# A cross-attention loop fused with two expert mixtures: each batch's turns, values and closing in the step behind its scores, and its row DMAs spread over more places

## The chip, the cores and the metric

The kernel runs on one core of a Trainium2 chip. The metric is the device time of one execution, in microseconds (us). The time of a kernel is the median of several runs. One more execution is recorded by the hardware profiler; its times are those of the profile.

## What is computed

Two layers work on x, 16 batches of 128 tokens by 256 features in float32, with a second sequence of the same shape as context. Cut to the parts that matter:

```python
x = x + tanh(g_xattn[0]) * mlstm(layernorm(x), ctx, ctx, ...)
x = x + tanh(g_ffn[0])   * mixture0(layernorm(x), ...)   # 8 experts, top 2, 2 shared experts
x = x + tanh(g_xattn[1]) * attention(layernorm(x), ctx, mask, ...)
x = x + tanh(g_ffn[1])   * mixture1(layernorm(x), ...)   # 16 experts in 4 groups, top 4, 1 shared expert

def attention(hq, hk, mask, Wq, bq, Wk, bk, Wv, bv):     # 16 heads of 16
    q, k, v = heads(hq @ Wq.T + bq), heads(hk @ Wk.T + bk), heads(hk @ Wv.T + bv)
    s = einsum('bhqd,bhkd->bhqk', q / sqrt(16), k) + (1 - mask)[:, None] * -10000.0
    return join_heads(einsum('bhqk,bhkd->bhqd', softmax(s), v))
```

The change touches only the third of these lines and what is woven into it: the end of mixture 0 (its rows are fetched back and added to x) and the beginning of mixture 1 (layer norm, shared expert, routing, sorting, and the scattering of rows to the experts' order).

## The kernel before

The stages follow each other: mLSTM and the shared experts of mixture 0; 39 tiles of mixture 0's experts; the attention loop, which this case is about; the expert tiles of mixture 1, a group of experts per tile, in two halves of the batches.

The 16 batches are in four groups g of GB = 4. The attention loop is a loop over steps b. Each engine executes its instructions in the order in which the program issues them, so the order of the calls in the loop is the order of the work ("manual schedule"); an engine waits at an instruction until what it needs is there. A step has these parts for a batch:

- scores(b): 16 matmuls of 32 rows each write four score tiles sp0 to sp3 in PSUM (L1001), four heads in each.
- softmax(b, r), r = 0 to 3: for each head, VectorE adds the mask and takes the row's extreme (L1014), then ScalarE takes the exponential (L1020). The result is a tile sc (7 buffers).
- turn(b, r): four TensorE transposes of sc into the PSUM tile tp (L1027), and a ScalarE copy to SBUF as pT (L1029, 4 buffers).
- values(b): 16 matmuls that use 32 columns of the array each, values times pT, into the PSUM tile cp (L1038), and a ScalarE copy as cT (L1043, 2 buffers). The values are widened by a column of ones, so that the row sums come along.
- close(b): four transposes of cT into the PSUM tile pv (L1051), on VectorE the reciprocal, a scaling and the product o (L1055 to L1058), and on GpSimd the addition of o to x (L1060).

In PSUM, the pool s3p has one buffer for each of sp0 to sp3, two buffers under the tag "tp" (tp, cp, pv, and the layer norm's ln_tp take turns in them) and two under the tag "e" (the results of big matmuls: qps, sgp, sup, yps, r1ps).

Into the steps, other work is woven as "units": at(step, place, (function, arguments)) files a unit under a step and one of its three places 0, 1, 2, and run(step, place) issues what is filed there. A place written as one number p stands for step p // 3, place p % 3. The units are:

- gather_b(b): two row DMAs on GpSimd (L678) that fetch mixture 0's rows of a batch; add_b(b): two VectorE operations that add them to x.
- ln_stats, apply3, ln_turn: a layer norm in three parts (VectorE and GpSimd; VectorE L324; transposes L336 on TensorE and copies L337 on ScalarE), once per group for the attention's queries ("q") and once for mixture 1 ("m").
- q_proj(g, o): four matmuls into qps (L985) and a VectorE operation (L989).
- shared4_gate: four matmuls into sgp (L1069) and a tanh on ScalarE (L1073). shared4_up: four matmuls into sup (L1079) and two VectorE operations, L1084 with the tanh and sgp, L1085 with sup; sgp's buffer is free after L1084. shared4_down: matmuls into yps (L1091) and a VectorE addition to x (L1095).
- pump(g): slices of the routing of a group (matmuls r1ps, L1103, a ScalarE operation, then a chain of VectorE operations). pump_sort(0): slices of the sorting of the first half's eight batches by expert group.
- scatter(0, k, j): a row DMA on GpSimd (L1254) that writes batch k's rows to their slots for one of two choices j. The first expert tile (xt, loaded by SyncE; transposed into xtp, L1286; multiplied, gu, L1301) reads what the scatters wrote.

In the kernel before, the step of scores(b) runs values(b-2) behind the scores, then in two halves: turn of two quarters of batch b-1, softmax of two quarters of batch b, and the units of one place; then close(b-2) and the units of place 2. So a batch takes part in three steps. SyncE's loads of keys, masks and values for later groups (L927, L931) are issued ahead of a step's scores.

The functions touched by the change and their callers:

Of the kernel before, what the change touches and what calls it, by code (L numbers as in the profile page):

```python
# [25 lines left out]
G = 4  # L26
GB = B // G
# [40 lines left out]
def flamingo_kernel(ctx: ExitStack, tc: tile.TileContext, a: dict, out: bass.AP):  # L68
# [87 lines left out]
    def tok(ap, g):  # L156
        return ap[g * GB : (g + 1) * GB].rearrange("b s d -> s b d")

    def bc(ap, shape):
        return ap.unsqueeze(len(shape) - 1).to_broadcast(shape)  # L160
# [540 lines left out]
    units = {}  # L701

    def at(step, place, *fs):
        units.setdefault((step, place), []).extend(fs)

    def run(step, place):
        for f, *args in units.pop((step, place), ()):
            f(*args)
# [7 lines left out]
    NB = G * GB  # L716
    ENG = {nc.tensor.engine, nc.vector.engine, nc.scalar.engine, nc.gpsimd.engine}
    for g in range(G):
        s0 = GB * g

        k1, k2 = (1, g), (2, g)
        s0 = GB * g - (g > 0)
# [8 lines left out]
        s0 = GB * g  # L731
# [164 lines left out]
    with tc.manual_schedule(engines=ENG):  # L896
        g = G - 1
# [24 lines left out]
    s3 = w3_stack.enter_context(tc.tile_pool(name="s3", bufs=2))  # L922
    s3p = w3_stack.enter_context(tc.tile_pool(name="s3p", bufs=1, space=PSUM))

    def load_k(g):
        kz_g[g] = s3.tile([P, KC, 2, TG], F32, tag="kz", name="kz")
        sync.dma_start(out=kz_g[g], in_=kz_d[g])  # L927

    def load_va(g, pr):
        va_g[g, pr] = s3.tile([P, 2, NH1, VW], F32, tag="va", name="va", bufs=3)  # L930
        sync.dma_start(out=va_g[g, pr], in_=va_d[g][:, 2 * pr : 2 * pr + 2])  # L931

    def new_mask():
        return s3.tile([P, GB, S], F32, tag="mb", name="mb")
# [31 lines left out]
    NR = P // VW  # L966
# [40 lines left out]
    def softmax(b, r, sp):  # L1007

        g, i = divmod(b, GB)
        sc = s3.tile([P, HQ, S], F32, tag="sc", name="sc", bufs=7)  # L1010
        mx = mx_b[b]
        for k in range(HQ):
            n = r * HQ + k
            nc.vector.tensor_tensor_reduce(  # L1014
                out=sc[:, k, :], in0=sp[:, k // 2, k % 2, :], in1=masks[g][:, i, :],
                scale=1.0, scalar=3.0e38, op0=ALU.add, op1=ALU.min, accum_out=mx[:, n : n + 1],
            )
        for k in range(HQ):
            n = r * HQ + k
            nc.scalar.activation(sc[:, k, :], sc[:, k, :], AF.Exp, scale=-1.0, bias=mx[:, n : n + 1])  # L1020
        sc_b[b, r] = sc

    def turn(b, r):
        sc = sc_b.pop((b, r))
        tp = s3p.tile([P, HQ, S], F32, tag="tp", name="tp", bufs=2)
        for k in range(HQ):
            nc.tensor.transpose(tp[:, k, :], sc[:, k, :], ident)  # L1027
        pT = s3.tile([P, HQ, S], F32, tag="pT", name="pT", bufs=4)
        nc.scalar.copy(pT, tp)  # L1029
        pT_b[b, r] = pT  # L1030

    def values(b):
        g, i = divmod(b, GB)
        cp = s3p.tile([P, NR, S], F32, tag="tp", name="cp", bufs=2)
        for r in range(NR):
            pT = pT_b.pop((b, r))
            for k in range(HQ):
                nc.tensor.matmul(  # L1038
                    cp[ts(k, VW), r, :], va_g[g, i // 2][:, i % 2, r * HQ + k, :], pT[:, k, :],
                    start=True, stop=True, tile_position=(0, k * VW),  # L1040
                )
        cT = s3.tile([P, NR, S], F32, tag="cT", name="cT")
        nc.scalar.copy(cT, cp)  # L1043
        cp_b[b] = cT

    def close(b):
        g, i = divmod(b, GB)
        cT = cp_b.pop(b)
        pv = s3p.tile([P, NH1, VW], F32, tag="tp", name="pv", bufs=2)
        for q in range(NR):  # L1050
            nc.tensor.transpose(  # L1051
                pv[:, ts(q, HQ), :].rearrange("p h d -> p (h d)"), cT[:, q, :], ident
            )
        rd = s3.tile([P, NH1], F32, name="rd")
        nc.vector.reciprocal(rd, pv[:, :, DH1])  # L1055
        nc.vector.tensor_scalar(rd, rd, tx1, None, ALU.mult)
        o = s3.tile([P, NH1, DH1], F32, name="o", bufs=1)
        nc.vector.tensor_tensor(o, pv[:, :, 0:DH1], bc(rd, [P, NH1, DH1]), ALU.mult)  # L1058
        xt = x_g[g][:, i, :]
        nc.gpsimd.tensor_tensor(xt, xt, o.rearrange("p h d -> p (h d)"), ALU.add)  # L1060
# [330 lines left out]
    for g in range(G):  # L1391
        q, m, s0 = ("q", g), ("m", g), GB * g
        for i in range(GB if g else 0):
            p = 3 * (s0 - 5) + i - 1 + 2 * (g == 1)
            at(*divmod(p, 3), (gather_b, s0 + i))
            at(*divmod(p + (4 if g == 1 else 2), 3), (add_b, s0 + i))
        if g == 0:
            at(-1, 0, (ln_turn, q, 0, s3p), (ln_turn, q, 1, s3p))
        else:
            n = 3 * (s0 - 3) + 2 * (g == 1)  # L1400
            at(*divmod(n, 3), (ln_stats, q, s3))
            at(*divmod(n + 1, 3), (apply3, q, 0))
            at(*divmod(n + 2, 3), (ln_turn, q, 0, s3p), (apply3, q, 1))
            at(*divmod(n + 3, 3), (ln_turn, q, 1, s3p))
        at(s0 - 1, 0, (q_proj, g, 0))
        at(s0 - 1, 1, (q_proj, g, 1))
        if g == G - 1:
            break
        at(s0 + 5, 2, (ln_stats, m, s3))
        at(s0 + 6, 0, (apply3, m, 0))  # L1410
        at(s0 + 6, 1, (ln_turn, m, 0, s3p), (apply3, m, 1))
        at(s0 + 6, 2, (ln_turn, m, 1, s3p))
        at(s0 + 7, 0, (shared4_gate, g, 0))
        at(s0 + 7, 1, (pump, g))
        at(s0 + 7, 2, (pump, g, 2))
        at(s0 + 8, 0, (pump, g, 2))
        at(s0 + 8, 1, (pump, g, 2))
        at(s0 + 8, 2, (pump, g))
        n = 3 * (s0 + 7) + 1
        for f in range(SC1):  # L1420
            at(*divmod(n + 2 * f, 3), (shared4_up, g, f))
            if f + 1 < SC1:
                at(*divmod(n + 2 * f + 1, 3), (shared4_gate, g, f + 1))
        n += 2 * SC1
        for t in range(0, GB, 2):
            at(*divmod(n + t // 2 - 1, 3), (shared4_down, g, t), (shared4_down, g, t + 1))
# [2 lines left out]
    ):  # L1429
        at(1 + b, 2, f)  # L1430

    at(13, 0, (pump_sort, 0, 1))
    at(13, 1, (pump_sort, 0, 2))
    at(13, 2, (pump_sort, 0, 2))
    at(14, 0, (pump_sort, 0, 2))
    at(14, 1, (pump_sort, 0, 2))
    for k in range(BH):
        at(14 + (k + 2) // 3, (k + 2) % 3, (scatter, 0, k, 0), (scatter, 0, k, 1))

    m = ("m", G - 1)
    at(GB * G + 1, 2, (ln_stats, m, s3))
    hooks = {
        0: [(apply3, m, 0), (apply3, m, 1)], 1: [(ln_turn, m, 0, s3p), (ln_turn, m, 1, s3p)],
        2: [(pump, G - 1, 1)], 3: [(pump, G - 1, 2)], 4: [(pump, G - 1, 2)], 5: [(pump, G - 1, 2)],
# [5 lines left out]
        hooks[NT1 + 4 + k] = [(gather, 0, k)]  # L1452

    with tc.manual_schedule(engines=ENG | {sync.engine}):
        for b in range(-1, NB + 3):
            if b >= 0 and b % GB == 0:
                if 0 < b < NB:
                    load_va(b // GB, 1)
            if b >= 0 and b // GB + 1 < G:
                g = b // GB + 1  # L1460
                if b % GB == 1:
                    load_k(g)
                elif b % GB == 2:
                    load_mask(g, new_mask())
                elif b % GB == 3:
                    load_va(g, 0)
            old = b - 1 if 0 < b <= NB else None
            sp = scores(b) if 0 <= b < NB else None
            if 0 <= b - 2 < NB:
                values(b - 2)  # L1470
            for hf in range(2):
                if old is not None:
                    turn(old, 2 * hf)
                    turn(old, 2 * hf + 1)
                for r in range(2 * hf, 2 * hf + 2):
                    if sp:
                        softmax(b, r, sp[r])
                run(b, hf)
            if 0 <= b - 2 < NB:
                close(b - 2)  # L1480
            run(b, 2)
    with tc.manual_schedule(engines=ENG):
        for i in range(NHF * NT1 + 2):
            tile_step(i)
            for f, *args in hooks.get(i, ()):
                f(*args)
        g, k = G - 1, 0
        for f in range(SC1):
            shared4_gate(g, f)
            shared4_up(g, f)  # L1490
            if f:
                gather(1, k)
                gather(1, k + 1)
                k += 2
        for t in range(GB):
            shared4_down(g, t)
            if k < BH:
                gather(1, k)
                k += 1
        for hf in range(NHF):  # L1500
            for g in range(hf * G // NHF, (hf + 1) * G // NHF):
                sync.dma_start(out=tok(out, g), in_=x_g[g])
# [83 lines left out]
```

## Time and profile before

| what | value |
|---|---|
| median of three runs | 984.41 us (980.81, 984.61, 984.41) |
| the profiled execution's own time | 979.63 us |
| its span in the profile | 977.9 us (1.7 us lie outside) |
| mean granted TensorE clock | 0.945 |
| instructions | 13890 |
| attention loop, first scores to the first matmul of mixture 1's tiles (gu) | 573.7 to 815.9 us, 242.2 us |
| length of the steps of scores 0 to 14 | 2.7, 7.8, 14.8, 14.8, 8.5, 11.1, 12.9, 23.1, 13.9, 14.5, 12.1, 15.9, 11.1, 13.3, 13.8 us |
| from the last scores to the first gu | 52.2 us |
| behind that, to the end | 162.0 us |

All times of the profile are counted from the start of the span. A step's length is the time from its first score matmul to the next step's. TensorE's row "PE" holds matmuls and "PEld" its weight loads, which lie beside matmuls; the granted clock is the part of full speed that TensorE was given, and at half clock (0.50) its matmuls take about twice as long. In a timeline line the numbers are the start, the duration of the stretch, the engine, the line, the operation, output and inputs, how many instructions the stretch holds, and in brackets how long the engine was idle before it and what released it.

### The profile page before, as it was taken

The numbers are of one execution on the slowest core, as the hardware profiler recorded it, in microseconds if no ns is written. First come the engines' busy times: TensorE is split into PE (matmuls) and PEld (weight loads), VectorE is DVE, ScalarE is ACT, GpSimd is POOL, SyncE is SP. The second block draws the span as 40 slices with busy tenths as digits, with TensorE's granted clock in tenths as the row PEclk, the third lists the DMA queues.
The fourth block names the chain that finished last, engine by engine and source line by source line (L and its number), as shares of the span: only waits on it lengthen the run. The fifth ranks groups of instructions, "written<-read, shape, count | busy, mean of one in ns | idle before, by whom it ended". The sixth has DMA issues, their size and how long they took to land. (4 is left out here: it accounts for less than half of the span.)

```text
span 977.9 us, 13890 instructions
## 1 busy us (share of the span) xinstructions
PE 860.3 (88%) x4432; PEld 535.9 (55%) x4432; DVE 472.2 (48%) x1731; ACT 394.0 (40%) x945; POOL 216.5 (22%) x316
## 2 busy tenths in 40 slices
PE   4778998999979999999999976768899679989996
PEld 2555556656545556566555644535656436555653
DVE  2496556554373222222222454838868344833634
ACT  2455655662102211211121145754666424444540
POOL 3023001110003111111110333231201241154515
PEclk9887999999999999999999977789999789999999
DMA  8998312100683111111110174120000012344613
GB/s 236 304 320 288 105 33 74 54 22 1 230 307 108 37 45 44 44 45 47 44 43 23 54 280 156 39 92 28 23 23 1 36 46 63 95 136 122 192 60 118
DMA packets 66390, 98.23 MB, mean 100 GB/s; under 512 B 9648, under 2 KB 49712, under 8 KB 65808
## 3 DMA queue, kind: packets, MB, share of 16 engines
q1 hardware_dynamic: 59840, 79.39, 24.8%
q0 software_dynamic: 6480, 17.97, 6.1%
q8 instruction: 37, 0.61, 0.3%
q14 instruction: 33, 0.27, 0.1%
HBM read 64.64 MB, written 32.69 MB: 100 GB/s over the span
## 5 line engine op out<-in xcount | busy, mean ns | idle before, releaser
L811 POOL DMA_INDIRECT xt<-xn_d,ti x39 | 39.8, 1021 | 209.5 <-PE xtp L826 164.3
L1020 ACT ACTIVATE sc<-sc,mx 128x128 f32<-128x128 f32 x256 | 78.3, 394 | 4.6 <-DVE mx L1014 4.6
L840 PE MATMUL tgp<-w1e,xT 128*128 x156 | 79.4, 593 | 0.0
L858 PE MATMUL typ<-w2e,thT 128*128 x312 | 76.9, 389 | 0.0
L1301 PE MATMUL gu<-wgu,xT 128*128 x152 | 73.8, 608 | 0.9 <-DVE xT L1288 0.5
L840 PE MATMUL tup<-w3e,xT 128*128 x156 | 73.3, 592 | 0.0
L858 PEld LDWEIGHTS typ<-w2e,thT 128*128 128x128 f32 x312 | 56.1, 189 | 31.2 <-ACT thT L855 25.1
L845 ACT ACTIVATE tsg<-tgp 128x512 f32<-128x512 f32 x39 | 23.3, 598 | 121.3 <-PE tgp L840 121.3
L847 DVE TENSOR_TENSOR h<-tup,tsg 128x512 f32<-128x512 f32 x39 | 27.0, 692 | 88.0 <-PE tup L840 85.4
L1027 PE MATMUL tp<-ident,sc 128*128 128x128 f32 x256 | 43.4, 310 | 28.1 <-ACT cT L1043 17.2
L519 PE MATMUL gp<-xnT,w 128*128 128x512 f32 x128 | 65.6, 636 | 0.0
L1014 DVE CUSTOM_DVE_ANT_0 sc<-sp,mb 128x128 f32<-128x128 f32 x256 | 56.3, 286 | 16.2 <-PE sp L1001 11.4
L530 PE MATMUL up<-xnT,w 128*128 128x512 f32 x128 | 60.8, 598 | 0.0
L540 PE MATMUL yp<-w,hT 128*128 128x256 f32 x256 | 58.4, 382 | 1.1 <-DVE hT L534 1.1
L862 DVE COPY ys<-typ 128x256 f32<-128x256 f32 x39 | 16.6, 426 | 87.5 <-PE typ L858 87.5
L1027 PEld LDWEIGHTS tp<-ident,sc 128*128 128x128 f32 x256 | 32.8, 159 | 44.7 <-ACT cT L1043 20.5
L534 DVE TENSOR_TENSOR hT<-up,sg 128x512 f32<-128x512 f32 x32 | 22.1, 691 | 69.6 <-PE up L530 39.7
L540 PEld LDWEIGHTS yp<-w,hT 128*128 128x128 f32 x256 | 47.7, 190 | 9.7 <-DVE hT L534 2.1
L678 POOL DMA_INDIRECT yg<-ys_d,si x32 | 33.5, 1047 | 85.9 <-DMA ys_d<-ys 43.0
L855 ACT COPY thT<-htp 128x512 f32<-128x512 f32 x39 | 22.9, 587 | 69.3 <-PE htp L853 69.3
L840 PEld LDWEIGHTS tup<-w3e,xT 128*128 128x128 f32 x156 | 29.6, 190 | 37.3 <-issue 37.1
L448 ACT ACTIVATE dm<-dm,gaT 128x128 f32<-128x128 f32 x128 | 40.5, 392 | 14.9 <-DVE dm L444 14.8
(281 smaller groups left out, 1600.8 us busy)
## 6 DMA issues: line engine op xcount, KB each, us to landing
dm<-m_d SPq DMA_DIRECT2D x16, 512.0 KB
xs<-zero SPq DMA_DIRECT2D x2, 2584.0 KB
xt<-xs SPq DMA_DIRECT2D x38, 136.0 KB
ys_d<-ys SPq DMA_DIRECT2D x39, 128.0 KB
ys<-ys SPq DMA_DIRECT2D x38, 128.0 KB
kz_d<-kst SPq DMA_DIRECT2D x8, 512.0 KB
va_d<-vs SPq DMA_DIRECT2D x8, 512.0 KB
w1e<-in_L_ffn_w_T_dram SPq DMA_DIRECT2D x8, 512.0 KB
```

Of the source, the lines that this page charges most:

```text
L448: nc.scalar.activation(t[:, h, :], t[:, h, :], AF.Exp, bias=gate_g[g][0][:, n : n + 1])
L519: nc.tensor.matmul(gp, shw[e][0][:, c, ts(f_, P)], xnT_g[2, g][:, c, :], start=(c == 0), stop=(c == KC - 1))
L530: nc.tensor.matmul(up, shw[e][1][:, c, ts(f_, P)], xnT_g[2, g][:, c, :], start=(c == 0), stop=(c == KC - 1))
L540: nc.tensor.matmul(yp, sh_g[g, e * HC0 + f][:, ts(t, P)], shw[e][2][:, f, :], start=(f == 0), stop=(f == HC0 - 1))
L678: nc.gpsimd.indirect_dma_start(out=yg, out_offset=None, in_=ys_d[:, :], in_offset=bass.IndirectOffsetOnAxis(ap=si_j[j][:, b : b + 1], axis=0),
L811: nc.gpsimd.indirect_dma_start(out=xt, out_offset=None, in_=xn_d[:, :], in_offset=bass.IndirectOffsetOnAxis(ap=ti[:, i : i + 1], axis=0), ...
L840: nc.tensor.matmul(ps, xT[:, c, :], w_[:, bass.ds(ev + c * HID0, HID0)], start=(c == 0), stop=(c == KC - 1),)
L858: nc.tensor.matmul(yp, hT[:, f, :], w2e[:, bass.ds(ev + f * D, D)], start=(f == 0), stop=(f == HC0 - 1))
L1014: nc.vector.tensor_tensor_reduce(out=sc[:, k, :], in0=sp[:, k // 2, k % 2, :], in1=masks[g][:, i, :], scale=1.0, scalar=3.0e38, op0=ALU.ad ...
L1020: nc.scalar.activation(sc[:, k, :], sc[:, k, :], AF.Exp, scale=-1.0, bias=mx[:, n : n + 1])
L1027: nc.tensor.transpose(tp[:, k, :], sc[:, k, :], ident)
L1301: nc.tensor.matmul(gu, xT[:, c, :], wgu[:, bass.ds(ev + c * NGRP * 2 * GW, 2 * GW)], start=(c == 0), stop=(c == KC - 1),)
```

## The change

Within the attention loop a batch takes part in two steps in place of three: in the step of scores(b) all four turns of batch b-1 follow the scores, then the softmax of three quarters of batch b, values(b-1), the fourth quarter's softmax, the units of places 0 and 1, close(b-1), and the units of place 2. The loop has one step fewer. On TensorE the order of a step is now scores, 16 transposes, cp's 16 matmuls, units, pv, units; before it was scores, cp's matmuls, 8 transposes, units, 8 transposes, units, pv, units. On ScalarE it is now four pT copies, twelve exponentials, cT, four exponentials, units; before it was cT, two pT copies, eight exponentials, units, two pT copies, eight exponentials, units.

The m units of the groups 0 to 2 (layer norm, shared expert, routing) are filed one step earlier, and the sort of the first half too. The q units stay where they are, so that in two steps a layer norm of each kind falls together. The gathers of groups 2 and 3 are filed at every second place, in place of four places in a row; those of group 1 stay. The 16 scatters are filed over ten places from step 13, place 2, to step 16, place 2; before, two were filed at each of eight places from step 14, place 2, to step 17, place 0. The last group's ln_stats is filed one step earlier. An assertion is added that no unit is left over.

```diff
@@ the filing of the units
-            p = 3 * (s0 - 5) + i - 1 + 2 * (g == 1)
+            p = 3 * (s0 - 6) - 1 + 2 * i if g > 1 else i - 2
             at(*divmod(p, 3), (gather_b, s0 + i))
             at(*divmod(p + (4 if g == 1 else 2), 3), (add_b, s0 + i))
...
-        at(s0 + 5, 2, (ln_stats, m, s3))
-        at(s0 + 6, 0, (apply3, m, 0))
-        at(s0 + 6, 1, (ln_turn, m, 0, s3p), (apply3, m, 1))
-        at(s0 + 6, 2, (ln_turn, m, 1, s3p))
-        at(s0 + 7, 0, (shared4_gate, g, 0))
-        at(s0 + 7, 1, (pump, g))
-        at(s0 + 7, 2, (pump, g, 2))
-        at(s0 + 8, 0, (pump, g, 2))
-        at(s0 + 8, 1, (pump, g, 2))
-        at(s0 + 8, 2, (pump, g))
-        n = 3 * (s0 + 7) + 1
+        at(s0 + 4, 2, (ln_stats, m, s3))
+        at(s0 + 5, 0, (apply3, m, 0))
+        at(s0 + 5, 1, (ln_turn, m, 0, s3p), (apply3, m, 1))
+        at(s0 + 5, 2, (ln_turn, m, 1, s3p))
+        at(s0 + 6, 0, (shared4_gate, g, 0))
+        at(s0 + 6, 1, (pump, g))
+        at(s0 + 6, 2, (pump, g, 2))
+        at(s0 + 7, 0, (pump, g, 2))
+        at(s0 + 7, 1, (pump, g, 2))
+        at(s0 + 7, 2, (pump, g))
+        n = 3 * (s0 + 6) + 1
...
-    at(13, 0, (pump_sort, 0, 1))
+    at(12, 0, (pump_sort, 0, 1))
+    at(12, 1, (pump_sort, 0, 2))
+    at(12, 2, (pump_sort, 0, 2))
+    at(13, 0, (pump_sort, 0, 2))
     at(13, 1, (pump_sort, 0, 2))
-    at(13, 2, (pump_sort, 0, 2))
-    at(14, 0, (pump_sort, 0, 2))
-    at(14, 1, (pump_sort, 0, 2))
     for k in range(BH):
-        at(14 + (k + 2) // 3, (k + 2) % 3, (scatter, 0, k, 0), (scatter, 0, k, 1))
+        for j in range(2):
+            at(*divmod(41 + (2 * k + j) * 10 // 16, 3), (scatter, 0, k, j))
...
-    at(GB * G + 1, 2, (ln_stats, m, s3))
+    at(GB * G, 2, (ln_stats, m, s3))
@@ the loop of the steps
-        for b in range(-1, NB + 3):
+        for b in range(-1, NB + 2):
...
-            if 0 <= b - 2 < NB:
-                values(b - 2)
-            for hf in range(2):
-                if old is not None:
-                    turn(old, 2 * hf)
-                    turn(old, 2 * hf + 1)
-                for r in range(2 * hf, 2 * hf + 2):
-                    if sp:
-                        softmax(b, r, sp[r])
-                run(b, hf)
-            if 0 <= b - 2 < NB:
-                close(b - 2)
+
+            if old is not None:
+                for r in range(NR):
+                    turn(old, r)
+            for r in range(NR - 1):
+                if sp:
+                    softmax(b, r, sp[r])
+            if old is not None:
+                values(old)
+            if sp:
+                softmax(b, NR - 1, sp[NR - 1])
+            run(b, 0)
+            run(b, 1)
+            if old is not None:
+                close(old)
             run(b, 2)
```

More of the change, by code (lines that the diff above doesn't have):

```diff
@@ L1486, in flamingo_kernel @@
                 f(*args)
+        assert not units
         g, k = G - 1, 0
```

## The prediction

> **What bounds the kernel now.** I read the busy table first, then the clock row, the table by stretch, the waits of the attention loop (566 to 816 us, the only part whose order the change alters), and last the timeline.
>
> The busy table says TensorE overall:
>
> ```profile
> PE 860.3 (88%) x4432; PEld 535.9 (55%) x4432; DVE 472.2 (48%) x1731; ACT 394.0 (40%) x945; POOL 216.5 (22%) x316
> PEclk9887999999999999999999977789999789999999
> ```
>
> Behind the opening slices, the clock digits under 9 are all in the attention loop. By stretch (us, busy PE, PEld, DVE, ACT, POOL with counts, granted clock, DMA share, GB/s):
>
> ```profile
> 646.20:669.30 23.10, 17.34 (x109) 10.19 (x108) 7.50 (x40) 8.99 (x25) 6.00 (x7) 0.85 0.33 109
> 709.70:725.60 15.90, 15.46 (x109) 9.20 (x108) 7.41 (x41) 8.79 (x25) 0.40 (x2) 1.00 0.12 34
> 763.70:815.90 52.20, 39.68 (x241) 25.22 (x240) 22.71 (x101) 15.14 (x34) 20.16 (x25) 0.84 0.15 51
> ```
>
> The middle row is a step in which TensorE is 97% busy at full clock; the others have the same kind of work, longer. In the waits the longest losses of ScalarE are at one copy, L1043, and TensorE then waits for that copy (about 38 us with weight loads counted apart from matmuls, overlapping):
>
> ```profile
> ACT cT L1043 <- remote: 31.7, 5, 8.4
> PEld tp L1027 <- ACT cT L1043: 20.5, 11, 5.7
> PE tp L1027 <- ACT cT L1043: 17.2, 6, 5.4
> ```
>
> "Remote" says only that the profile doesn't know the releaser. The timeline does. Two places, batch 5 and batch 14:
>
> ```profile
> 646.48 1.17 POOL L678 DMA_INDIRECT yg<-ys_d,si  x1 [0.16 <-issue]
> 647.29 1.08 PE L1038 MATMUL cp<-pT,va 128*32 128x128 f32 x32
> 651.92 1.01 POOL L678 DMA_INDIRECT yg<-ys_d,si  x1 [0.30 <-issue]
> 653.75 0.59 ACT L1043 COPY cT<-cp 128x512 f32<-128x512 f32 x1 [6.68 <-remote]
> 655.29 3.35 PE L1069 MATMUL sgp<-xnT,wsh 128*128 128x512 f32 x4
> ```
>
> ```profile
> 784.97 1.08 PE L1038 MATMUL cp<-pT,va 128*32 128x128 f32 x32
> 791.41 0.98 POOL L1254 DMA_INDIRECT xs<-xr,si  x1 [0.31 <-issue]
> 792.12 0.59 ACT L1043 COPY cT<-cp 128x512 f32<-128x512 f32 x1 [6.45 <-remote]
> 793.66 3.62 PE L1079 MATMUL sup<-xnT,wsh 128*128 128x512 f32 x4
> ```
>
> The value products cp take 1.08 us, but their copy starts when GpSimd's train of row DMAs (1.0 us each, one per 1.3 us) is over. From cp's start to cT's start it is 1.12 us for batches 7 to 12 (no train beside them), and 5.1, 6.4, 3.4, 7.3, 7.1, 3.2 us for batches 1, 5, 6, 13, 14, 15, which have one. Against 1.12 (1.98 at half clock, batches 1 and 13) the excess is 3.1+5.3+2.3+5.4+6.0+2.1, with 0.4 at batch 2 **24.6 us**. After each long one the four matmuls of sgp or sup take 3.35 to 3.62 us against 1.88: half clock, about 2 to 3 us of lost matmul time each, **8 to 11 us** in all.
>
> **The change part by part.** (a) *Row DMAs spread.* Gathers of batches 8 to 15 go from trains of 5 and 3 to pairs, 2.6 us, at every second place (those of batches 4 to 7 stay); the 16 scatters are spread over ten places, but GpSimd takes them in order and only its adds (L1060) stand between, so they are still trains of 5, 5, 5, 1. DMAs and counts are the same. Cost on GpSimd nil: in the steps it waits 107.6 us for o. The sort and routing are issued one step sooner, so scatter 0 is ready; the last scatter comes after the last close, and the first expert tile's load stands behind it: before, that load had 3.5 us to spare against yps; I put 0 to 1 us.
>
> (b) *Values behind all four turns.* The cp of a batch starts 4.75 us after the step's scores instead of 1.1. Work it out for one full-clock step: scores 1.15; 16 transposes in two tp buffers that ACT empties at 0.59 (pitch 0.53): TensorE idles about 0.9 us there (0.3 before), cp ends at 4.75. ScalarE: four pT copies end at 4.2, twelve exponentials of 0.307 at 7.9, cT at 8.5, four exponentials at 9.7, and only then the first tanh, at 10.3. Before, eight exponentials were followed by the units. So behind cT on ScalarE stand 4 exponentials, the tanh L1073 and the xnT copies; DVE's L1084 waits for the tanh, and with it the "e" buffer (two) that the third big matmul of the step needs.
>
> For a step with sgp, ln_tp, r1ps, sup, pv, sgp: sgp to 6.5, ln_tp 6.9, r1ps 8.7, then sup waits for L1084 (10.3+0.7=11.0), idle 2.3; 12.7; pv 13.1; sgp 14.8; with the 0.5 us of small gaps that such steps show now, 15.3. The same walk gives 16.7 for (sup qps sgp qps pv sup), 14 to 14.5 for (sgp sup pv yps), 14 to 14.9 for (yps and both layer norms, which now fall in one step): 60.5 for four steps. Now the four steps from 709.7 to 763.7 take 54.0. That is +6.5 per four steps, two such periods: **+13**. Bounds: 0 (units as well covered as now) to +20 (every step waits for its tanh twice).
>
> (c) *One step fewer.* The last step's chain is gone, and a batch's values and close stand one step sooner, so step 1 grows by about 5.5 us.
>
> Sum by stretch, in the profiled run (span 977.9, the run 979.63):
> - 573.7 to 646.2: now 72.5; less 3.5 stall and 3 half clock, plus 5.5 (step 1), plus 0.6 coupling in five steps: 75.5, and step 3 and 4's loads as now: 74.5.
> - 646.2 to 763.7: now 117.5; less 7.6 stall and 4 half clock, plus 13: 119.
> - 763.7 to the first gu at 815.9: now 52.2; less 13.5 stall and 4 half clock: 34.7; less a step of 6: 28.7. The stalls of batches 13 to 15 can't come back at their full length: a train of 5 ends 6.5 us into the step, cp done by about 7.2, and cT has its turn on ScalarE only at 7.9. Bounds 0 to 6 us back; I take 0.
>
> Together 222.2 against 242.2: **-20**. New idle stretches of 2.3 us bring half-clock windows: see below, **+5**. So 964.6 for the profiled run, -15.0; on the median 984.41, which lies 4.8 above the profiled run, **969.4, say 970**.
>
> **Two rules weighed.** The Trainium skill, "SBUF — State Buffer", section "Who interferes with whom", says that a DMA never contends with a compute engine and that TensorE waits on no one. By it the trains would not be the cause and the cp delay would stay: then cT comes at 8.5 at the earliest in any case, so of delays of 5.1 to 7.3 us some 1 to 3.7 remain each, 12 us over five, plus their half clock 3: 985. The rows (six of six long ones beside a train, none of six without one) decide; I keep the rule as a rival. "TensorE: Matmul & The Clock Gate", section "Why this matters for your kernels", allows idle gaps up to about 3 us before the clock halves. By it the 2.3 us gaps are free (965). The rows: the idle time 619.11 to 621.26 (2.15) was followed by half clock from 620.7 to 627.5, that before L1091 at 693.53 (1.57) was not. So two steps in four may pay, 6.8 us at half clock costing up to 3.4 each: 0 to 14, I take 5. The same page, "Part 4: PE-mode transpose", says that transposes don't count as busy for the clock; then 16 in a row would look idle in every step, some 2.5 us lost in 16 steps, 1005. The row against it, all transposes but one gap, at clock 1.00:
>
> ```profile
> 704.87 0.60 PE L1027 MATMUL tp<-ident,sc 128*128 128x128 f32 x4
> 705.70 0.66 PE L1027 MATMUL tp<-ident,sc 128*128 128x128 f32 x4 [0.24 <-ACT xnT L337]
> 706.20 0.66 PE L336 MATMUL ln_tp<-ident,xr 128*128 128x128 f32 x4
> 707.09 0.66 PE L1051 MATMUL pv<-ident,cT 128*128 128x128 f32 x4 [0.24 <-ACT pT L1029]
> ```
>
> **The rivals.** *Likeliest (0.45):* as summed, 970, own range 958 to 979. *Coupling hidden (0.13):* the steps keep their 13.5 us, -13: 957. For it: 97% busy steps now, against it: ScalarE's order, which has no slack in the walk. *No change (0.22):* the trains are not the cause, or they hold turns and scores as well as cp, so the stalls stay: 984. For it: the trains of 5 scatters remain; against it: the scores beside a train at 764 had their DVE readers start on time. *Slower (0.20):* half clock. Where TensorE is idle over some 2 us in a step (between 1.57 and 2.15 by the rows), the window at half clock follows; the eight heavy steps, six of which run at 1.00 now, would each lose up to 3.4 us: 27, of which 5 is counted: 970+22=992. It decides at the third big matmul, the one that waits for the tanh.
>
> **How the numbers follow.** An effect under 0.5% (4.9 us) can't be told from no change here. Faster by more (below 979.5): the likeliest and the hidden case, with a little of "no change": 0.60. Same: 0.20. Slower: 0.20. The range takes the likeliest, the hidden case and half of the slower: 953 to 995.
>
> **What would show it.** Right: cp to cT never over 4.5 us with ScalarE idle; no "cT <- remote" above 10 us in the waits; first gu near 796 to 801; tanh at 10 us in the heavy steps, with idle time before the third big matmul of 2 us; heavy periods of 60 us. Wrong: cp to cT still 5 us and more with idle ScalarE beside a single pair of row DMAs (the cause was another); clock below 0.9 in the stretch that is now at 1.00 (the slower rival); periods of 54 (coupling hidden).

## The result, and the profile after

The changed kernel takes 987.38 us (median of 17 runs, 981.26 to 992.77) beside 981.98 us for the kernel before in as many runs: the ratio is 1.0066, 95% interval 1.0042 to 1.0089. It is slower by about 5 us, where 14 fewer had been forecast. The profiled execution spans 991.1 us; its attention loop, first scores to first gu, has 248.8 us against 242.2. It was the slowest of the 17 (992.77), while the profiled one of before was 2.4 us under its median, so the two profiles are 13.2 us apart where the medians are 5.4: 6.6 of them in the loop, 3.3 ahead of it and 3.3 behind it.

The busy table and the clock row of the changed kernel:

```profile
PE 873.2 (88%) x4432; PEld 541.5 (55%) x4432; DVE 474.1 (48%) x1731; ACT 393.7 (40%) x945; POOL 216.2 (22%) x316
PEclk9797999999999999999999978779889989999998
```

The counts are those of before: the same work, in 13 us more of busy TensorE. Where the kernel before had four slices at 9 in the second half of the loop (behind its 7778), the changed one has 9, 8, 8, 9.

In the waits of the loop (engine, line, who it waited for: us in total, times, longest), the late cT is no longer among the longest (cT <- remote fell from 31.7 to 1.0 us):

```profile
ACT pT L1029 <- PE tp L1027: 59.7, 39, 7.9
DVE hs L1084 <- ACT th L1073: 36.2, 6, 7.4
PEld pv L1051 <- ACT cT L1043: 11.7, 6, 3.7
```

In its place stand waits of ScalarE for transposes (14.0 us in the kernel before), of VectorE for the tanh (4.7 before), and of the closing transposes for cT. The changed kernel has about the same three waits on the second occasion described below (54.8, 31.7 and 11.5 us), so they belong to its order. One heavy step of the changed kernel, scores 10, in its timeline:

```profile
713.68 3.61 ACT L1020 ACTIVATE sc<-sc,mx 128x128 f32<-128x128 f32 x12
717.20 0.57 ACT L1043 COPY cT<-cp 128x512 f32<-128x512 f32 x1
717.66 1.28 ACT L1020 ACTIVATE sc<-sc,mx 128x128 f32<-128x128 f32 x4
718.84 0.58 ACT L1073 ACTIVATE th<-sgp 128x512 f32<-128x512 f32 x1
719.78 0.23 ACT L1110 ACTIVATE scr<-r1ps 128x64 f32<-128x64 f32 x1
720.06 3.78 PE L1079 MATMUL sup<-xnT,wsh 128*128 128x512 f32 x4 [1.58 <-ACT scr L1110]
```

This is the queue on ScalarE that the prediction walked through: twelve exponentials, cT, four, tanh, and TensorE's third big matmul waits behind it, by the profile for the last operation of the queue (scr) rather than for the tanh's reader L1084. It then takes 3.78 us in place of 1.88: half clock.

The same count for every run, worked out from the traces, is used below. "Idle" is the time of the loop in which neither a matmul nor a weight load is shown, "half" the time at a granted clock of 0.50, and "work" is loop less idle less half of "half" (matmuls take twice as long there, so half of that time is lost).

| first profiles | loop | idle | half | work | scores 6 to 9 | 10 to 13 | 14 | last scores to gu |
|---|---|---|---|---|---|---|---|---|
| before | 242.2 | 51.6 | 61.4 | 159.9 | 64.3 | 52.3 | 13.8 | 52.2 |
| changed | 248.8 | 49.8 | 64.9 | 166.5 | 67.8 | 64.9 | 17.0 | 36.3 |

The end gained 16 us, more than the whole gain forecast; the steps ahead of it lost more than that. And trains of scatters hold more than cp. Step 15 of the changed kernel:

```profile
790.61 1.10 PE L1027 MATMUL tp<-ident,sc 128*128 128x128 f32 x8
791.25 0.97 POOL L1254 DMA_INDIRECT xs<-xr,si  x1 [0.30 <-issue]
792.86 0.59 ACT L1029 COPY pT<-tp 128x512 f32<-128x512 f32 x1 [2.61 <-PE tp L1027]
793.49 0.66 PE L1027 MATMUL tp<-ident,sc 128*128 128x128 f32 x4 [1.78 <-issue]
793.81 0.97 POOL L1254 DMA_INDIRECT xs<-xr,si  x1 [0.30 <-issue]
794.34 0.59 ACT L1029 COPY pT<-tp 128x512 f32<-128x512 f32 x1 [0.90 <-PE tp L1027]
```

The copy of the transposes began 2.25 us after their start; here the turns are held up as the values were before. A train holds a cp as well, that of the last batch, behind which no exponentials of a next batch stand:

```profile
808.91 1.21 PE L1038 MATMUL cp<-pT,va 128*32 128x128 f32 x32
812.90 0.97 POOL L1254 DMA_INDIRECT xs<-xr,si  x1 [0.30 <-issue]
813.52 0.59 ACT L1043 COPY cT<-cp 128x512 f32<-128x512 f32 x1 [3.88 <-PE sgp L1069]
```

From cp to cT it is 4.6 us, with ScalarE idle; on the second occasion the same place takes 1.15 us.

### The profile page after: what moved, and what is told of

It is laid out like the page before. It is cut to its first block, busy times and chain, and to the rows that moved or that the text cites. A ratio compares the mean times of both kernels' runs of the same rounds, so it can differ in the third digit from the quotient of the medians.

```text
span 991.1 us, 13899 instructions
## 1 busy us (share of the span) xinstructions
PE 873.2 (88%) x4432; PEld 541.5 (55%) x4432; DVE 474.1 (48%) x1731; ACT 393.7 (40%) x945; POOL 216.2 (22%) x316
## 5 line engine op out<-in xcount | busy, mean ns | idle before, releaser
L1029 ACT COPY pT<-tp 128x512 f32<-128x512 f32 x64 | 35.9, 587 | 60.0 <-PE tp L1027 59.7
L540 PEld LDWEIGHTS yp<-w,hT 128*128 128x128 f32 x256 | 47.8, 190 | 9.0 <-issue 1.6
L840 PEld LDWEIGHTS tup<-w3e,xT 128*128 128x128 f32 x156 | 29.6, 190 | 37.3 <-issue 37.1
L678 POOL DMA_INDIRECT yg<-ys_d,si x32 | 33.4, 1042 | 62.1 <-DMA ys_d<-ys 43.0
```

Of the source, the lines that this page charges most:

```text
L540: nc.tensor.matmul(yp, sh_g[g, e * HC0 + f][:, ts(t, P)], shw[e][2][:, f, :], start=(f == 0), stop=(f == HC0 - 1))
L840: nc.tensor.matmul(ps, xT[:, c, :], w_[:, bass.ds(ev + c * HID0, HID0)], start=(c == 0), stop=(c == KC - 1),)
```

## The experiments

All of them ran on another occasion than the first runs (the expectations call it "this place"), and there the kernel before takes 951 us, 31 less; every ratio below is against the kernel before on that occasion. The experiments' runs were on two chips, with 951 us on both; on which chip the first runs were is not on record.

**The kernel before, for its trace on this occasion.** No edit.

> The kernel before itself, for its trace in this place. If the held-back signals are absent: cp to cT 1.12 us at full clock beside trains of row DMAs too, the loop 213 to 217 us in place of 242, the last stretch 36. If they are a property of the program: cp to cT 5 to 7 us for batches 5, 13 and 14 as in its first profile.

One run, 950.93 us. Batch 13, in its timeline:

```profile
755.18 0.98 POOL L1254 DMA_INDIRECT xs<-xr,si  x1 [0.30 <-issue]
755.82 1.08 PE L1038 MATMUL cp<-pT,va 128*32 128x128 f32 x32
756.47 0.97 POOL L1254 DMA_INDIRECT xs<-xr,si  x1 [0.30 <-issue]
756.97 0.59 ACT L1043 COPY cT<-cp 128x512 f32<-128x512 f32 x1 [2.48 <-PE cp L1038]
757.75 0.98 POOL L1254 DMA_INDIRECT xs<-xr,si  x1 [0.30 <-issue]
```

The same train at the same pitch, and cT begins 1.15 us after cp in the middle of it. The loop is 213.3 us: 28.9 of the first profile's 242.2 are not a property of the program, and 28.8 of them lie in the stretches of the long late copies (step 3: 14.8 against 10.0 us, step 7: 23.1 against 15.9, from the last scores to gu: 52.2 against 35.4). A train of row DMAs alone does not hold TensorE's signals back; something that belonged to the first occasion did so beside the trains.

**The changed kernel on this occasion.** No edit.

> The changed kernel itself, beside the other runs. If the held-back signals are absent again, as in the runs so far in which the kernel before took 952 us: theory (the order costs 20 to 25 us, which the stalls' removal nearly paid for where they occurred): 972 to 977 us, 2 to 2.6% over the kernel before. Rival (the change costs the same 5 us everywhere): 957.

969.77 us, ratio 1.0199 (1.0169 to 1.0229): 2 us under the theory's range, 13 over the rival's 957. Loop 235.5. So the change costs 22.2 us of loop (19 of the whole) where nothing is held back, and it cost 6.6 in the first profiles because 15.6 us of what the first occasion added went away: of 28.9 in the kernel before, 13.3 (248.8 less 235.5) were still there in the changed kernel. 9.8 of them are in steps 14 to 16 with their trains; the other 3.5 are in steps 6 to 13, where idle time is the same on both occasions and half clock is 10.3 us more.

**Only the row DMAs spread**, in the old order and filling.

```diff
-            p = 3 * (s0 - 5) + i - 1 + 2 * (g == 1)
+            p = 3 * (s0 - 6) - 1 + 2 * i if g > 1 else i - 2
...
-        at(14 + (k + 2) // 3, (k + 2) % 3, (scatter, 0, k, 0), (scatter, 0, k, 1))
+        for j in range(2):
+            at(*divmod(44 + (2 * k + j) * 10 // 16, 3), (scatter, 0, k, j))
```

> The old order of a step and the old filling, with only the gathers of groups 2 and 3 at every second place and the 16 scatters over ten places. Theory (a train of row DMAs holds back the signals of TensorE that fall beside it): the stalls of batches 5 and 6 go, 7.6 us and 4 to 5 us of half clock behind them, while the scatters stay trains and keep theirs: 10 to 12 us under the kernel before. Rival (the row DMAs are not the cause of the late cT copies): no change, within 3 us.

951.97 us, 1.0011 (0.9989 to 1.0032): no change. With no stalls on this occasion there was nothing to take away, so this says that spreading is free, and not what it brought on the first occasion.

**The scatters left out**, from the kernel before and from the changed one; the experts of the first half then work on zeros, so only the time says something.

> The kernel before without the 16 scatters of the first half (left out, so its experts work on zeros). Theory (trains hold back TensorE's signals): the stalls of batches 13 to 15, 13.5 us, and about 4 us of half clock go: 15 to 18 us under the kernel before. Rival (row DMAs are not the cause): 0 to 3 us under.

950.24 us, 0.9987 (0.9973 to 1.0002).

> The changed kernel without the 16 scatters of the first half (left out, so its experts work on zeros). Theory (trains of scatters hold back the turns as well as the values in steps 14 to 16): from the last scores to gu 36.3 goes to 27 to 29 us, step 14 from 17.0 to 15, so 9 to 11 us under the changed kernel. Rival (ScalarE's order alone makes the tail long): 0 to 3 us under.

971.46 us, 1.0208 (1.0156 to 1.0260), the time of the changed kernel with scatters. Both expectations of the theory fell: on this occasion the trains cost nothing that shows in either order.

**Where the 22 us of the loop come from.** Against the kernel before on this occasion, idle grew by 13.6, half clock by 10.3 (5.2 us of matmul time), work by 3.5. Four trials, first one at a time.

*The two layer norms apart*, the queries' of groups 2 and 3 two places later:

```diff
-            n = 3 * (s0 - 3) + 2 * (g == 1)
+            n = 3 * (s0 - 3) + 2
```

> The changed kernel with the layer norm of the queries two places later, so that it no longer falls into the step of the other layer norm. Theory (two layer norms in one step leave TensorE with several gaps of 1 to 1.6 us, and the half clock that follows makes steps 6 and 10 longer): steps 6 and 10 back to 15.5 us from 19.2 and 19.5, so 6 to 8 us under the changed kernel. Rival (the half clock comes from the gaps that ScalarE's order opens in every heavy step): the half clock only moves, within 2 us of the changed kernel.

973.41 us, 1.0226 (1.0202 to 1.0249), 4 us over the changed kernel. Steps 6 and 9 fell from 19.2 to 17.7 and from 14.6 to 11.5, steps 10 and 12 took it back (18.0 and 19.0 against 16.2 and 17.7); half clock in the loop 47.8 against 44.4. The half clock moved, as the rival said, though the whole is 4 us off and not within its 2.

*ScalarE's order*: cT behind eight exponentials, the units of place 0 ahead of the last eight.

```diff
-            for r in range(NR - 1):
+            for r in range(2):
                 if sp:
                     softmax(b, r, sp[r])
             if old is not None:
                 values(old)
-            if sp:
-                softmax(b, NR - 1, sp[NR - 1])
             run(b, 0)
+            for r in range(2, NR):
+                if sp:
+                    softmax(b, r, sp[r])
             run(b, 1)
```

> The changed kernel with cT behind eight exponentials in place of twelve, and the units of place 0 ahead of the last eight; TensorE's order is the same. Theory (ScalarE's order opens the idle times: the tanh and cT stand behind sixteen exponentials): the four steps of scores 10 to 13 go from 64.9 to 56 to 58 us, idle from 10.6 to 6 or less and half clock from 11.8 to 0 to 4; the whole 12 to 18 us under the changed kernel. Rival (the block of sixteen transposes on TensorE costs it): within 3 us of the changed kernel.

965.79 us, 1.0142 (1.0106 to 1.0177): 4 us of the 12 to 18. Steps 10 to 13 in 61.4 us, idle 10.1 against 10.8.

*The halves kept*: two turns, two softmaxes and the units, twice, as before, and the values behind the fourth turn (the added lines alone):

```diff
+            for hf in range(2):
+                if old is not None:
+                    turn(old, 2 * hf)
+                    turn(old, 2 * hf + 1)
+                    if hf:
+                        values(old)
+                for r in range(2 * hf, 2 * hf + 2):
+                    if sp:
+                        softmax(b, r, sp[r])
+                run(b, hf)
```

> The changed kernel with the two halves of before kept (two turns, two softmaxes, units, twice), the values behind the fourth turn, everything else as changed: one step fewer, filling and scatters as changed. Theory (the order within the step costs it, not the shorter span of a batch): steps 10 to 13 in 53 to 56 us and from the last scores to gu 28 to 30: 8 to 12 us under the kernel before. Rival (a batch in two steps costs it, whatever the order: close waits for a cT of its own step): as the changed kernel, 960 to 975.

968.23 us, 1.0182 (1.0165 to 1.0199). The theory fell once more: with the old order of a step, steps 10 to 13 still take 63.2 us. The trace shows a different wait, though. Step 11 of this kernel:

```profile
715.99 1.88 PE L1079 MATMUL sup<-xnT,wsh 128*128 128x512 f32 x4
719.68 0.17 DVE L1153 FIND_INDEX8 i<-m,sb 128x8 uint32<-128x16 f32 x1
720.12 0.67 DVE L1084 SCALAR_TENSOR_TENSOR hs<-th,sgp 128x512 f32<-128x512 f32 x1
720.84 2.50 PE L985 MATMUL qps<-xnT,wq 128*128 128x512 f32 x4 [2.97 <-DVE hs L1084]
```

The tanh was there at 714.7; L1084 came at 720.1, since VectorE was in the routing's chain of small operations. Its buffer was awaited by qps, the projection of the queries, which the shifted filling puts into this very step: the m units were moved by a step, the q units not. VectorE has 13.6 us of work in this step and 6.9 and 8.0 in its neighbours.

*The queries' units moved along* (and two of the four gathers of a group one place forward), with the changed order:

```diff
-            p = 3 * (s0 - 6) - 1 + 2 * i if g > 1 else i - 2
+            p = 3 * (s0 - 6) - 1 + (0, 2, 3, 5)[i] if g > 1 else i - 2
...
-            n = 3 * (s0 - 3) + 2 * (g == 1)
+            n = 3 * (s0 - 4) if g > 1 else 3 * (s0 - 3) + 2
...
-        at(s0 - 1, 0, (q_proj, g, 0))
-        at(s0 - 1, 1, (q_proj, g, 1))
+        at(s0 - 1 - (g > 1), 0, (q_proj, g, 0))
+        at(s0 - 1 - (g > 1), 1, (q_proj, g, 1))
```

> The changed kernel with only the queries' layer norm and projection of groups 2 and 3 moved one step forward along with the second mixture's units. Theory A: steps 10 to 13 from 63 to 65 down to 56 to 58, steps 6 to 9 likewise: 953 to 958. Rival B (ScalarE's and TensorE's order): within 4 us of the changed kernel's 970.

971.23 us, 1.0211 (1.0164 to 1.0258): nothing gained, 62.1 us for steps 10 to 13. That alone, too, is no cure.

**Both at once.** The halves kept and the queries' units moved along:

> The halves kept and the new filling, with the queries' layer norm and projection of groups 2 and 3 moved one step forward too, so that q and m units stand to each other as before. Theory A: steps 6 to 9 and 10 to 13 in 53 to 56 us each, the last stretch 29: 938 to 945, under both kernels. Rival B: steps 10 to 13 stay at 60 to 63, 960 to 968.

955.30 us, 1.0037 (1.0022 to 1.0051). Steps 6 to 9 in 55.4 and 10 to 13 in 55.8 us. In the table of stretches (us, busy PE, PEld, DVE, ACT and POOL, clock, DMA share, GB/s), steps 10 to 13 of the kernel before on this occasion, of the changed one, of the moved units alone, of the halves alone, and of both:

```profile
685.64:739.58 53.94, 49.51 (x376) 31.98 (x375) 37.09 (x212) 34.25 (x93) 5.49 (x8) 0.97 0.03 11
```

```profile
700.67:764.04 63.37, 52.44 (x376) 32.98 (x375) 41.37 (x233) 33.40 (x92) 5.52 (x8) 0.95 0.03 9
```

```profile
700.40:762.50 62.10, 51.74 (x371) 32.04 (x370) 39.97 (x230) 32.83 (x91) 5.43 (x8) 0.95 0.03 9
```

```profile
698.00:761.22 63.22, 51.92 (x375) 33.31 (x375) 40.64 (x231) 33.48 (x92) 5.67 (x10) 0.93 0.03 9
```

```profile
692.90:748.70 55.80, 47.68 (x375) 30.77 (x374) 39.97 (x230) 33.26 (x92) 5.62 (x10) 0.99 0.04 11
```

Either cause alone is enough for 62 to 63 us in these four steps: mending one gives at most 1.3 us, mending both 7.6. In steps 6 to 9 they come nearer to adding: one gives 3.4 or 4.4, both 10.3. The whole is still 0.4% over the kernel before. The same with the old filling in place of the moved one. The changed order with the filling of before:

> The changed kernel's order of a step with the filling of the kernel before: the second mixture's units, the sort and the scatters stand where they stood, the loop has its last step again (without attention). Theory A (the shifted filling costs it: the projection of the queries now falls into the step of the routing's long chain on VectorE, and the two layer norms into one step): the four steps of scores 10 to 13 in 56 to 58 us, as against 63 to 65 with the new filling and 52 to 54 before. Rival B (the order of the calls costs it): 60 to 63. The whole, with a tail of 34: 955 by A, 965 by B.

976.37 us, 1.0247 (1.0201 to 1.0294); steps 10 to 13 in 62.4, as rival B said, the whole 11 us over its 965. And the halves with the filling of before:

> The same with the two halves of a step kept, values behind the fourth turn. Theory A: steps 10 to 13 in 53 to 55 us (61 to 63 with the new filling), the whole 948 to 953, as the kernel before. Rival B (closing a batch in the step of its turns costs it): 58 to 62, 958 or more.

959.06 us, 1.0078 (1.0055 to 1.0102); steps 10 to 13 in 53.4 as theory A said, the whole over its range by 6 us. Against the kernel before, the loss is in the first six steps (59.3 us against 53.2) and the last stretch (41.1 against 35.4).

**Which engine's order.** e6's order with the queries' units moved along, so that the filling can't hide it:

> The order of e6 (TensorE's as changed, on ScalarE cT behind eight exponentials and the units of place 0 ahead of the last eight) with the queries' norm and projection moved along as in e11 and e12. Theory (ScalarE's order is what the changed order costs): steps 6 to 9 and 10 to 13 in 54 to 57 us each as with the halves kept (55.4 and 55.8), 953 to 957. Rival (the block of sixteen transposes): 60 to 62 as in e12, 964 to 970.

963.69 us, 1.0129 (1.0085 to 1.0173), between the two: 59.8 and 60.4 us for the two groups, where all sixteen transposes in a row and ScalarE's late cT give 62.3 and 62.1, and the halves 55.4 and 55.8. The rival said 60 to 62, the theory 54 to 57. ScalarE's late cT and units are worth about 2 us of the 6 to 7; the rest stays with the sixteen transposes in a row, which put their four copies in a row on ScalarE too, so it is not TensorE's alone. The count of the loops:

| second occasion | loop | idle | half | work | scores 0 to 5 | 6 to 9 | 10 to 13 | 14 | last scores to gu |
|---|---|---|---|---|---|---|---|---|---|
| before | 213.3 | 31.7 | 34.1 | 164.5 | 53.2 | 56.6 | 53.9 | 14.2 | 35.4 |
| changed | 235.5 | 45.3 | 44.4 | 168.0 | 62.9 | 65.7 | 63.4 | 14.1 | 29.4 |
| ScalarE's order (e6) | 228.5 | 41.3 | 41.0 | 166.7 | 60.3 | 63.9 | 61.4 | 14.2 | 28.6 |
| halves (e7) | 229.7 | 42.5 | 47.8 | 163.3 | 60.5 | 61.3 | 63.2 | 15.5 | 29.2 |
| q along (e12) | 232.5 | 42.8 | 44.4 | 167.5 | 64.4 | 62.3 | 62.1 | 14.2 | 29.6 |
| halves, q along (e11) | 220.1 | 36.7 | 41.0 | 162.9 | 62.1 | 55.4 | 55.8 | 17.5 | 29.3 |
| old filling (e9) | 240.0 | 45.6 | 54.6 | 167.1 | 60.2 | 64.2 | 62.4 | 12.7 | 40.5 |
| halves, old filling (e10) | 221.9 | 38.2 | 41.0 | 163.2 | 59.3 | 54.4 | 53.4 | 13.7 | 41.1 |
| ScalarE's order, q along (e14) | 225.2 | 37.5 | 41.0 | 167.2 | 62.7 | 59.8 | 60.4 | 13.7 | 28.6 |

In this table the kernels with sixteen transposes in a row have 166.7 to 168.0 of "work", those with halves 162.9 to 164.5. The matmuls are the same; the 4 us may be waits that no trace shows as idle, between transposes that go through two buffers and ScalarE's copies. That is not shown, and kernels of one order differ by 2.5 us among themselves (162.0 in the run with only the row DMAs spread, 164.5 in the kernel before).

**Better ends.** Two steps per batch only from step T = 4 on, with the queries' units moved along, and only from T = 12 on, in the filling of before with the row DMAs spread and with group 2's m units alone one step earlier. In both, the step of the switch closes two batches (shown against the loop of the halves kept):

```diff
+            if 0 <= b - 2 and b <= T:
+                values(b - 2)
             for hf in range(2):
...
-                    if hf:
+                    if hf and b >= T:
                         values(old)
...
+            if 0 <= b - 2 and b <= T:
+                close(b - 2)
-            if old is not None:
+            if old is not None and b >= T:
                 close(old)
```

> e11 with three steps per batch up to step 3 and two from step 4 on (both batches are closed in step 4). Theory (where nothing fills the steps, closing a batch in the step of its turns shows as idle time): steps 0 to 5 from 62 down to 54 to 57 us, the whole 947 to 951. Rival (those steps are held by transfers and half clock): 60 to 62, 955.

959.07 us, 1.0080 (1.0058 to 1.0101). Steps 0 to 5 stay at 61.8: the 4.7 us that step 1 gives back turn up in step 2 (16.4 against 13.8) and step 5 (13.7 against 11.5). The theory on the first steps fell; what they lose to is not settled. They hold units that were moved forward, and half clock (25.2 us against 20.5 in the kernel before).

> The kernel before up to step 11 (with the spread gathers), from step 12 two steps per batch with the halves kept, and only the last group's units of the second mixture one step earlier. Theory (the changed step's only gain is at the end, 6 us, since the last batch is closed one step sooner; all else costs): loop 209 to 212 as against 213.3, the last stretch 29 to 31, 945 to 949: 0.3 to 0.6% under the kernel before. Rival (the step in which two batches are closed, and the fuller steps behind it, take the gain): 951 to 955.

967.87 us, 1.0175 (1.0142 to 1.0209). Steps 10 to 13, with the one in which two batches are closed, have 60.9 us (53.9 before) and step 14 has 17.1 (14.2), as the rival said. The last stretch has 38.8 us in place of the 29 to 31 expected:

```profile
796.33 0.97 POOL L1254 DMA_INDIRECT xs<-xr,si  x1 [0.30 <-issue]
800.98 1.26 PE L1286 MATMUL xtp<-ident,xt 128*128 128x128 f32 x4 [9.48 <-DMA xt<-xs]
```

The sort and the scatters were left at the places of the kernel before, spread to the end, so the last scatter ended at 797.3, and TensorE stood idle for the first tile. No version tried is faster than the kernel before.

## Why the prediction was wrong, point by point

**"Sum by stretch": the removal of the stalls, -35.6 us with their half clock, is the step that failed.** It was taken as complete ("Bounds 0 to 6 us back; I take 0"). Measured by the two occasions, 15.6 us went. The 20.0 missing are of two kinds. There was less to remove: 28.9 us, half clock included, and not 35.6. And 13.3 stayed: 9.8 in steps 14 to 16, over the bound of 6, and 3.5 of half clock in other steps. The prediction saw that the scatters stay trains of 5, but let them touch only cp, hidden behind ScalarE's exponentials. In the first profile of the changed kernel they hold the turns of step 15, which nothing hides, and the cp of batch 15, which has no exponentials to hide behind. The rival "they hold turns and scores as well as cp" named it for the turns; its price was set at no change.

**The cost of the order, 20.6 us, was right in size.** The prediction took 35.6 off 242.2, which leaves 206.6, and reached 227.2 with +5 for half clock. Measured where nothing is held back: 213.3 and 235.5, 22.2. Term by term: the two groups of heavy steps +13 and +5 of half clock against 9.1+9.5=18.6; step 1 +5.5 against 5.3; the last stretch -6 against -6.0; the other early steps +3.0 (0.6 in each of five; with it the line's 74.5 comes out, its 75.5 does not) against 4.4. So 20.0 of the 21.6 us by which the loop was missed are the stalls, 1.6 the order. These are single traces; steps 10 to 13 of the kernel before differ by 1.6 us between its two.

**The mechanism of that cost was half right.** The queue on ScalarE is in the trace as walked through: in steps 6 to 14 the tanh of the step's first sgp comes 9.3 to 13.5 us behind the first scores (forecast 10.3), and in steps 6 and 10 the third big matmul waits 1.7 and 1.6 us (forecast 2.3). The cp, which the text has at 4.75 us once as its start and once as its end, ended there 4.9 us into a full-clock step. But the prediction laid the +13 on ScalarE's order. The runs give 2 us of 6 to 7 to ScalarE's late cT and units, the rest to the block of transposes and their copies, and show a second cause of about the same size that it had passed over: the projection of the queries meeting the routing's chain on VectorE, since one set of units was moved and the other not. It had counted the two layer norms in one step, and not the queues of VectorE in the step behind. In steps 10 to 13 the two do not add.

**The rivals.** *No change* (984) was nearest in number, by luck: it rested on stalls that stay, and the record has stalls of which half went and an order that cost more than that. *Slower* (992, half clock) was near too, and its sign appeared: step 10 ran at a clock of 0.70. It is part of the loss and not the whole: half clock in the loop grew by 3.5 us in the first profiles and by 10.3 on the second occasion, 1.8 to 5.2 us of matmul time, and by 11.8 in steps 10 to 13 of the first profiles, 5.9 us, not 27. What the prediction borrowed from the row at 619.11, that one gap over some 2 us decides, is also too simple: the clock fell at 620.7, when that gap was 1.6 us long. In the changed kernel's table of stretches, at the end of step 9:

```profile
701.00:704.00 3.00, 1.32 (x9) 0.84 (x8) 2.64 (x10) 1.67 (x5) 0.00 (x0) 1.00 0.00 0
704.00:707.00 3.00, 1.04 (x6) 0.80 (x7) 2.01 (x7) 0.58 (x1) 1.35 (x2) 0.79 0.00 0
707.00:710.00 3.00, 3.00 (x22) 1.86 (x21) 1.95 (x7) 0.59 (x1) 2.05 (x3) 0.50 0.01 3
```

TensorE was 44% and 35% busy in two stretches of 3 us, and the clock fell at 705.8, behind gaps of 0.99 and 1.65 us. So the clock fell without a gap of the about 3 us that the Trainium skill gives ("TensorE: Matmul & The Clock Gate", section "Why this matters for your kernels"). What fits is the busy share. The clock of these traces changes in steps of 3.41 us (half clock lasts 3.41, 6.83 or 10.24 in the two first profiles). Here are three slots of that length: ahead of this fall, ahead of the fall at 620.7 in the kernel before, and one of the kernel before, of transposes alone, behind which the clock stayed at 1.00:

```profile
702.35:705.76 3.41, 1.63 (x12) 1.07 (x11) 2.65 (x11) 0.68 (x2) 1.07 (x2) 1.00 0.00 0
617.29:620.70 3.41, 1.63 (x12) 1.03 (x10) 3.37 (x26) 3.15 (x11) 1.99 (x2) 1.00 0.26 70
706.03:709.45 3.42, 1.79 (x15) 1.28 (x13) 2.89 (x19) 3.11 (x11) 0.38 (x1) 1.00 0.01 2
```

TensorE's matmuls fill 48%, 48% and 52% of them. Counted over the attention loops of all 17 traces, the clock fell behind 98 of the 106 full-clock slots that matmuls fill to less than 50%, and behind 35 of the 791 others; these 35 are not explained. Transposes have to be counted as busy for this: without them the best dividing line puts 86 of the 897 slots on the wrong side, with them 38. This is a count of what went together; no run changed the share alone.

**The Trainium skill's rule that a DMA does not contend with a compute engine** ("SBUF — State Buffer", section "Who interferes with whom") was set aside on six coincidences against six. On the second occasion the trains are there and hold nothing, so the trains are not sufficient, and the rule stands there. What held TensorE's signals on the first occasion is open: in the loop it appeared only beside row DMAs, it did not come back in any later run, and so nothing could be tried on it.

## What to carry to other kernels

A stall that coincides with something is explained only when the coincidence without the stall has been looked for in a second execution elsewhere; before one removes it, ask for that trace. When woven work is moved, every set of units has its place relative to the others, on every engine's queue: moving one set and not the next can cost as much as a bad order, and since either can be enough to make a step late, undoing one of two causes can show nothing. The closing of a batch in the step of its turns gained 6 us once, at the end, with the moved filling (29.4 against 35.4); in every version that did so from the start, the first six steps took 6 to 12 us more (59.3 to 64.9 against 53.2).

## What was not expected of the hardware

The same kernel took 982 us on one occasion and 951 on another, its spread within each under 1.1%, with cp to cT of 1.15 to 7.3 us in the one and 1.15 to 2.2 in the other. And the clock of TensorE halved behind gaps of 0.99 and 1.65 us, at a busy share of 48% over 3.41 us.
